# Rows of AUGRU steps 4 to 11: eight gathers of whole rows and a spread by plain DMAs, in place of 32 gathers of quarter rows; other PSUM banks for the first AUGRU products

## The chip, the cores and the metric

One core of a Trainium2 chip runs the whole program in one launch. The metric is the device time in microseconds (us). The kernel before takes 2016.64 us (median of 3 runs, 2015.94 to 2016.9). Its profiled execution, from which every row below comes, has a span of 1995.2 us from its first to its last instruction.

Engines are named as in the profile: PE (TensorE), DVE (VectorE), ACT (ScalarE), POOL (GpSimd, which also issues the indirect DMAs) and SP (SyncE, which here issues all other DMAs but two).

## The reference

A recommender of the DIEN kind: a GRU over 100 steps, an attention over its states, a second GRU whose update gate is scaled by the attention (AUGRU), and a small network at the end. The batch is 1024, every width is 128.

```python
_, gru_seq = jax.lax.scan(gru_step, h0, jnp.swapaxes(item_historical_embedding, 0, 1))
keys = jnp.swapaxes(gru_seq, 0, 1)                       # (1024, 100, 128)
q = jnp.broadcast_to(item_embedding[:, None, :], keys.shape)
feat = jnp.concatenate([keys, q, keys - q, q * keys], axis=-1)
score = _mlp(feat, [(att_W0, att_b0), (att_W1, att_b1), (att_W2, att_b2)], jax.nn.relu)
score = jnp.where(mask[:, :, None] == 1, score, -jnp.inf)
attn = jax.nn.softmax(score, axis=1)[..., 0]
pooled = jnp.einsum('bt,btd->bd', attn, keys)
att_seq = pooled.T[:T]                                   # row t: one weight for each batch entry

def augru_step(h, inp):
    x_t, a_t = inp
    ti = jnp.concatenate([h, x_t], axis=-1)
    r = jax.nn.sigmoid(ti @ aug_Wr.T + aug_br)
    u = jax.nn.sigmoid(ti @ aug_Wu.T + aug_bu)
    h_hat = jnp.tanh(jnp.concatenate([h * r, x_t], axis=-1) @ aug_Wh.T + aug_bh)
    u = a_t[:, None] * u
    h_new = (1.0 - u) * h + u * h_hat
    return (h_new, h_new)
_, aug_seq = jax.lax.scan(augru_step, h0, (jnp.swapaxes(keys, 0, 1), att_seq))
idx = (sequential_length - 1)[:, None, None]
attention_feature = jnp.take_along_axis(jnp.swapaxes(aug_seq, 0, 1), idx, axis=1)[:, 0, :]
```

The AUGRU reads at step t the state of the first GRU at step t (its key, `x_t`) and one attention weight for each batch entry (`a_t`). Only the state at a sequence's last step is used, so a sequence that has ended need not be carried further.

## The kernel before, in words

The 1024 batch columns are two halves of 512. Instructions stand in each engine's queue in the order in which the program writes them (`manual_schedule`); each engine takes its own queue in order, and waits at an instruction until the semaphores that it needs have come.

**First phase** (`gru_phase`, 0 to about 1406 us). 100 GRU steps for both halves, with attention scores, the softmax and the pooling beside them. The states are transposed in 32x32 blocks into tiles `kt` and stored to DRAM tables `keys_d[q]`: `keys_d[0]` holds steps 0 to 3, each further one eight steps (`keys_d[1]`: steps 4 to 11). The batch entries are ranked by length meanwhile.

**Second phase** (`augru_phase`, from about 1406 us to the end). The batch is now in the order of the ranks, so that the columns in use shrink from 510 at step 1 to a few at the end. A step is taken for half 0 and then half 1 (`half_step(t, i)`, written (t, i) below). For (t, i) the PE closes three products that were opened with the key (`open_gates`, L1264) by adding the state's part (`close_gate`, L1268): `pr`, `pu`, and later `ph` with r*h. ACT makes the sigmoids (L1292, L1293) and the tanh (L1276), DVE the products: r*h (L1300), u times the attention weight `at` (L1305), (u-1)*h (L1308), and in the next half step the new state (L1298, L1302).

Three kinds of data have to arrive by DMA:

- **keys.** The rows of `keys_d[q]` are gathered in rank order by indirect DMAs of 128 rows. For steps 0 to 3 a gathered row is one batch entry. For the later ones a gathered row is a quarter of an entry (32 of the 128 features of 8 steps, 1 KB), placed so that DVE can transpose it by 32x32 blocks into a key (`load_key`, L1253). 16 gathers serve a half's eight steps. For steps 4 to 11 half 0's are issued in three lots (four at step T-2, four after the loop, eight at the end of the phase), half 1's sixteen after the gathers of the attention weights. The keys of step 4 are read at (3, 0) and (3, 1).
- **attention weights of steps 1 to 3** (`chosen`). They come from a product on the PE; `store_chosen` copies them (L1199) and SP stores them to DRAM (`att_d<-att_t`, L1200) and loads them back, spread over the partitions (`at<-att_d`, L1228), for steps 2 and 3.
- **attention weights of the later steps.** SP stores the pooled features (`pooled_d<-pooled`, L1146); POOL gathers them in rank order (`att_r`, L158); DVE masks them (L1206), PE transposes them (`pw`, L1213), and SP stores and loads them in the same way (L1216, L1228).

Every DMA that SP issues has one of eight semaphores in turn, and the framework lets it wait until the DMA eight places before it has landed; the same holds for POOL's indirect DMAs with eight others.

PSUM has eight banks. In the second phase seven of them go round in a ring (`NEXT_BANKS`, then `LATE_BANKS`); the products of (1, 0) take `LATE_BANKS` by name, the first copy of weights takes `SPARE`. A bank is free for them when its last use in the first phase has ended, which for some is the DVE's pooling at the very end (L699, L700).

## Time and profile before

| | |
|---|---|
| time of the timed runs, median (lowest to highest) | 2016.64 us (2015.94 to 2016.9) |
| profiled execution, first to last instruction | 1995.2 us |
| difference of the two, outside the instructions | 21.4 us |
| PE busy, share of the span | 1980.5 us, 99% |
| DVE, ACT, POOL busy | 1673.4, 940.7, 1262.7 us |
| PE's share of the chain that ended last | 98% |
| indirect DMAs of rows (L193) | 218, 972 ns of POOL each |
| SP's DMAs of the weights `at<-att_d` (L1228) | 196, 319 to 589 ns of issue each |

How to read it. A row of the timeline has its start in us from the first instruction, its duration in us, the engine, the line, the operation, what it writes and reads, and the count of instructions merged into it; in square brackets stands how long the engine sat idle before it, and what ended that. SPq is SP issuing a DMA: its duration is that of the issue and not of the transfer. A row of waits has the engine and line that waited, on whom, the total in us, the number of times and the longest. A row of the table by stretches has the stretch, then each engine's busy time in it, the granted PE clock, the mean busy share of the 16 DMA engines and GB/s.

### The profile page before, as it was taken

The page shows a single profiled execution, that of the slowest core. Times are in us where ns is not written, and L with a number is a line of the kernel's source. Part 1 is how long each engine was busy: PE and PEld are TensorE (multiplying, and loading weights), DVE is VectorE, ACT ScalarE, POOL GpSimd, SP SyncE. Part 2 cuts the span into 40 slices and gives each one's busy share as a digit, 9 for nine tenths or more (in the row PEclk, how much of TensorE's full clock was granted, in tenths as well). Part 3 has the DMA queues.
Part 4 walks back from the last instruction along what each step waited for, and adds up shares of the span by engine and source line. Part 5 has one row for each costly group of instructions (what it writes and reads, how often), then busy time and mean ns, then how long its engine had stood idle before and what let it go on. Part 6 is the DMA issues. An engine that isn't in the chain of part 4 may idle for free.

```text
span 1995.2 us, 40926 instructions
## 1 busy us (share of the span) xinstructions
PE 1980.5 (99%) x15324; PEld 877.7 (44%) x15324; DVE 1673.4 (84%) x3036; ACT 940.7 (47%) x1689; POOL 1262.7 (63%) x1300
## 2 busy tenths in 40 slices
PE   9999999999999999999999999999999999999998
PEld 2333333333333333333333333334444556678997
DVE  7888999887979898888888798998687778888995
ACT  4444454454544444544545444446334444445553
POOL 0333939669796959496796858898763354445331
PEclk9999999999999999999999999999999999999999
DMA  4443333223334434332343333332543333333331
GB/s 125 99 119 92 108 105 102 89 84 108 116 104 113 116 99 134 111 106 85 103 129 108 93 107 108 92 108 67 155 146 92 96 111 97 93 103 100 83 81 35
DMA packets 244572, 205.59 MB, mean 103 GB/s; under 512 B 61811, under 2 KB 207068, under 8 KB 244364
## 3 DMA queue, kind: packets, MB, share of 16 engines
q1 hardware_dynamic: 231852, 170.31, 29.5%
q0 software_dynamic: 12224, 32.05, 5.7%
q8 instruction: 122, 2.00, 0.4%
q14 instruction: 86, 0.70, 0.1%
q10 hardware_dynamic: 288, 0.52, 0.1%
HBM read 146.75 MB, written 54.42 MB: 101 GB/s over the span
## 4 chain that ended last, share of the span: by engine, by line
PE 98%; DVE 1%; ACT 0%; issue 0%; ACTq 0%; DVEq 0%
PE ps L588 51%; PE pm L770 18%; PE ph L1268 5%; PE pr L1264 4%; PE pu L1264 4%; PE ph L1264 4%; PE pu L1268 4%; PE pr L1268 4%; PE last L737 1%; PE pr L1359 0%; PE ph L1359 0%; PE p L1479 0%; ACT pr L1378 0%; PE pd L248 0%; DVE r L1386 0%
## 5 line engine op out<-in xcount | busy, mean ns | idle before, releaser
L588 PE MATMUL ps<-x,wih 128*32 128x512 f32 x4800 | 603.2, 593 | 0.0
L588 PE MATMUL ps<-hn,whh 128*32 128x512 f32 x4752 | 597.1, 592 | 0.0
L588 PEld LDWEIGHTS ps<-x,wih 128*32 128x32 f32 x4800 | 175.6, 110 | 342.7 <-issue 338.1
L588 PEld LDWEIGHTS ps<-hn,whh 128*32 128x32 f32 x4752 | 173.7, 110 | 338.2 <-issue 335.6
L600 ACT ACTIVATE r<-ps,brz 128x512 f32<-128x512 f32 x200 | 137.5, 688 | 381.3 <-PE ps L588 381.1
L573 POOL TENSOR_TENSOR xm<-x,m 128x512 f32<-128x512 f32 x200 | 233.3, 1167 | 66.7 <-DMA m<-mask_d 66.5
L574 POOL TENSOR_TENSOR hist<-hist,xm 128x512 f32<-128x512 f32 x200 | 258.2, 1291 | 15.7
L193 POOL DMA_INDIRECT rows<-keys_d,idx_k x218 | 212.0, 972 | 84.0 <-POOL rows L192 69.2
L700 POOL TENSOR_TENSOR pooled<-pooled,kw 128x512 f32<-128x512 f32 x192 | 245.5, 1279 | 15.1
L699 POOL TENSOR_TENSOR kw<-kt,e 128x512 f32<-128x512 f32 x192 | 206.3, 1074 | 67.9 <-DVE e L888 67.9
L621 ACT ACTIVATE ps<-ps,bih 128x512 f32<-128x512 f32 x198 | 131.1, 662 | 228.4 <-DVE ps L618 228.4
L770 PE MATMUL pm<-hn,wk 128*32 128x512 f32 x1200 | 215.0, 592 | 0.0
L770 PE MATMUL pm<-kq,wkq 128*32 128x512 f32 x1200 | 214.9, 592 | 0.0
L1276 ACT ACTIVATE c<-ph,bh 128x510 f32<-128x510 f32 (+57 forms) x174 | 88.3, 507 | 252.0 <-PE ph L1268 251.5
L608 DVE SCALAR_TENSOR_TENSOR u<-ps,bhh,r 128x512 f32<-128x512 f32 x198 | 147.4, 744 | 68.5 <-PE ps L588 66.3
L770 PE MATMUL pm<-mv,w 128*32 128x512 f32 (+1 forms) x808 | 194.9, 592 | 0.1
L631 DVE TENSOR_TENSOR d<-hn,ps 128x512 f32<-128x512 f32 x198 | 136.0, 687 | 36.0 <-ACT ps L621 35.7
L618 DVE TENSOR_TENSOR ps<-ps,u 128x512 f32<-128x512 f32 x200 | 140.0, 700 | 24.1 <-PE ps L588 3.1
L642 ACT COPY hn<-ps 128x512 f32<-128x512 f32 x198 | 115.4, 583 | 92.5 <-DVE kq L637 90.8
L632 DVE TENSOR_TENSOR d<-ps,d 128x512 f32<-128x512 f32 x198 | 136.9, 691 | 26.2 <-ACT ps L622 11.0
L192 POOL COPY rows<-rest 128x1 f32<-128x1 f32 x186 | 35.0, 188 | 192.8 <-DVE rest L1308 191.1
L1298 DVE TENSOR_TENSOR pu<-pu,c 128x510 f32<-128x510 f32 (+57 forms) x173 | 81.9, 473 | 77.8 <-ACT c L1276 75.5
(271 smaller groups left out, 3138.9 us busy)
## 6 DMA issues: line engine op xcount, KB each, us to landing
x<-in_hist_x SPq DMA_DIRECT2D x210, 256.0 KB
keys_d<-kt SPq DMA_DIRECT2D x48, 1024.0 KB
m<-mask_d SPq DMA_DIRECT2D x200, 128.0 KB
rows<-keys_d,idx_k POOLq DMA_INDIRECT x218, 3.0
s_b<-mv SPq DMA_DIRECT2D x200, 8.0 KB
keys_d<-kt SPq DMA_DIRECT2D x32, 64.0 KB
mask_i<-in_mask SPq DMA_DIRECT2D x8, 200.0 KB
part_d<-part SPq DMA_DIRECT2D x2, 400.0 KB
```

Source lines behind the costliest of these rows:

```text
L193: nc.gpsimd.indirect_dma_start(out=r[:, at, :], out_offset=None, in_=keys_d[q], in_offset=bass.IndirectOffsetOnAxis(ap=idx_k[:, k, i : i + ...
L573: nc.gpsimd.tensor_mul(d, x, m)
L574: nc.gpsimd.tensor_add(acc, acc, d)
L588: nc.tensor.matmul(p[ts(q, R), :], lhsT=w[:, g, ts(q, R)], rhs=v, start=(j == 0), stop=(j == len(parts) - 1),)
L600: nc.scalar.activation(r, pr, AF.Sigmoid, bias=brz[:, 0:1])
L608: nc.vector.scalar_tensor_tensor(out=u, in0=ph, scalar=bhh[:, 2:3], in1=r, op0=ALU.add, op1=ALU.mult,)
L618: nc.vector.tensor_add(pi, pi, u)
L699: eng.tensor_mul(d, k, w)
L700: eng.tensor_add(acc, acc, d)
L770: nc.tensor.matmul(p[i][s, :], lhsT=w[:, s], rhs=v, start=start, stop=stop)
L1264: nc.tensor.matmul(p, lhsT=m[:, 1, :], rhs=k, start=True, stop=False)
L1268: nc.tensor.matmul(p, lhsT=m[:, 0, :], rhs=v, start=False, stop=True)
```

## The change

Five things change.

1. `keys_d[1]` is laid out by whole batch entries (row: 8 steps x 128 features, 4 KB), where it was by quarters. `store` writes it with four DMAs (one for each 32 partitions) where it was one.
2. The 16 gathers of half 0 for steps 4 to 11 become four gathers of 128 whole rows (512 KB each), all after the pooling, into tiles `pair`. `spread_rows` then moves each gathered tile to the places that DVE reads, by 16 DMAs from SBUF to SBUF of 32 partitions x 1 KB, issued by SP: 64 DMAs.
3. The same for half 1: gathers of groups 0 and 1 stand before the gathers of the attention weights and are spread at once (32 DMAs of SP), those of groups 2 and 3 after them, spread at (2, 0) (32 more). They go through two buffers (`st3`).
4. `LATE_BANKS` is (4, 0, 5) and no longer (2, 4, 5), `SPARE` is 2 and no longer 0, and the ring has bank 2 where bank 0 was. The ring is the same but for the names of three banks.
5. The tile `part3` of the last prediction has one buffer (room for `st3`).

```diff
--- before.py
+++ after.py
@@ -75,7 +75,7 @@
 WIDTHS = [[max(LEAST, n) for n in alive] for alive in ALIVE]
 
 FREE = 134 * 256
-LATE_BANKS, SPARE, NEXT_BANKS = (2, 4, 5), 0, (6, 3, 1, 0)
+LATE_BANKS, SPARE, NEXT_BANKS = (4, 0, 5), 2, (6, 3, 1, 2)
 
 PR = P // NH
 BQ = B // (P // R)
@@ -115,7 +115,7 @@
     dram = ctx.enter_context(tc.tile_pool(name="dram", bufs=1, space=DRAM))
 
     keys_d = [
-        dram.tile([B, n * P] if q < WHOLE else [NK * P, n * R], F32, name=f"keys_d{q}")
+        dram.tile([B, n * P] if q <= WHOLE else [NK * P, n * R], F32, name=f"keys_d{q}")
         for q, n in enumerate(READ)
     ]
@@ -164,6 +164,21 @@
 
     rows = {}
 
+    def part_of(q, i, k):
+        some = rows[q, i]
+        part, at = divmod(k, KH // len(some))
+        return some[part], at
+
+    def spread_rows(i, g, whole):
+
+        to, at = part_of(WHOLE, i, g * P // R)
+        for k in range(P // R):
+            for p in range(P // R):
+                nc.sync.dma_start(
+                    out=to[ts(p, R), at + k, :],
+                    in_=whole[ts(k, R), ts(p, READ[WHOLE] * R)],
+                )
+
     def load_rows(q, i, width, tiles):
 
         n = READ[q]
@@ -179,14 +194,14 @@
             tiles.tile([P, KH // parts, n * R], F32, tag=tag, name="rows") for _ in range(parts)
         ]
         rows[q, i] = some
+        if q == WHOLE:
+            return
         for k in range(-(-width // R)):
             load_row(q, i, k)
             yield
 
     def load_row(q, i, k):
-        some = rows[q, i]
-        part, at = divmod(k, KH // len(some))
-        r = some[part]
+        r, at = part_of(q, i, k)
         if later.get("pace") is not None:
 
             nc.gpsimd.tensor_copy(r[:, at, 0:1], later["pace"])
@@ -666,6 +681,16 @@
 
             def store(self, q):
                 row, part = divmod(q - WHOLE, 2)
+                if row == 0:
+                    to = keys_d[WHOLE][self.cols, :].rearrange(
+                        "(k r) (p m) -> p r k m", r=R, p=P // R
+                    )
+                    for p in range(P // R):
+                        nc.sync.dma_start(
+                            out=to[p][:, :, ts(part, G * R)],
+                            in_=self.kt[q][ts(p, R)].rearrange("p k n c -> p k (n c)"),
+                        )
+                    return
                 nc.sync.dma_start(
                     out=keys_d[WHOLE + row].rearrange("(k p) m -> p k m", p=P)[
                         :, self.ks, ts(part, G * R)
@@ -929,12 +954,6 @@
 
         rest = load_later()
         early = [load_rows(0, i, HB, mid) for i in range(NH)]
-        more_early = load_rows(1, 0, HB, kx)
-
-        def gather_early(n):
-            for _ in range(n):
-                next(more_early)
-
 
         late, again, early_from = 6, 24, 84
         for s in range(T):
@@ -1001,8 +1020,6 @@
                 if last:
                     half.cross_features()
 
-            if s == T - 2:
-                gather_early(4)
             for half in halves:
                 half.pool(2 if len(half.todo) > 7 or s >= 92 else 1, nc.gpsimd)
                 if s >= GATHER:
@@ -1026,7 +1043,6 @@
             for f in these:
                 next(features[f])
 
-        gather_early(4)
         some(0, 1)
         take(T - 2)
         for half in halves:
@@ -1148,7 +1164,15 @@
                 )
         halves[0].kt[q] = kept
         halves[0].store(q)
-        all_of(more_early)
+        all_of(load_rows(WHOLE, 0, HB, kx))
+        wholes = []
+        for g in range(GH):
+            if g % 2 == 0:
+                pair = kp.tile([P, 2, READ[WHOLE] * P], F32, tag="kt", name="pair")
+            wholes.append(pair[:, g % 2, :])
+            gather(wholes[g], keys_d[WHOLE], g, 0)
+        for g in range(GH):
+            spread_rows(0, g, wholes[g])
 
     def augru_phase(pools, widths, alive):
 
@@ -1157,6 +1181,7 @@
         qp = pools.enter_context(tc.tile_pool(name="qp3", bufs=4 * NH))
         wp = pools.enter_context(tc.tile_pool(name="wp3", bufs=3))
         sp = pools.enter_context(tc.tile_pool(name="sp3", bufs=2))
+        st = pools.enter_context(tc.tile_pool(name="st3", bufs=2))
         kp = pools.enter_context(tc.tile_pool(name="kp3", bufs=4))
 
         minus = [wp.tile([P, P], F32, name=f"minus{j}", bufs=1) for j in range(2)]
@@ -1430,7 +1455,7 @@
                     in_offset=i and bass.IndirectOffsetOnAxis(ap=idx_p[:, g : g + 1], axis=0),
                 )
 
-            part = sp.tile([P, M0], F32, tag=f"part_{tag}", name="part3")
+            part = sp.tile([P, M0], F32, tag=f"part_{tag}", name="part3", bufs=1 if last else 2)
             rows_of(part, part_d, None, True)
             yield
             f0 = sp.tile([MC, n, P], F32, name="f0")
@@ -1545,11 +1570,24 @@
         chosen = [later["chosen", i] for i in range(NH)]
         keys.update({(1, i): later["key", 1, i] for i in range(NH)})
         open_gates(1, 0, ("pr", "pu"), LATE_BANKS)
+        all_of(load_rows(WHOLE, 1, HB, kp))
+
+        wholes = {}
+
+        def gather_wholes(*groups):
+            for g in groups:
+                wholes[g] = st.tile([P, READ[WHOLE] * P], F32, name="whole")
+                gather(wholes[g], keys_d[WHOLE], g, 1)
+
+        def spread_wholes(*groups):
+            for g in groups:
+                spread_rows(1, g, wholes.pop(g))
+
+        gather_wholes(0, 1)
+        spread_wholes(0, 1)
         sorted_rows = [gather_weights(i) for i in range(NH)]
-        ahead = load_rows(1, 1, widths[FIRST[1]], kp)
-        for _ in range(P // R):
-            next(ahead)
-        due = spread_over(-(-widths[FIRST[1]] // R) - P // R, NH * (FIRST[1] - 2))
+        gather_wholes(2, 3)
+        due, ahead = [], iter(())
         jobs, final = [], None
         for t in range(1, T):
             if t == one:
@@ -1563,6 +1601,8 @@
                     half_step(t, i)
                 elif i == 0:
                     whole_step(t)
+                if (t, i) == (2, 0):
+                    spread_wholes(2, 3)
                 for _ in range(due.pop(0) if due else 0):
                     next(ahead, None)
 
```

The order of SP's queue, where the first phase ends and the second begins (`pooled_d` is the store of the pooled features, `keys_d_72` that of the last block of states, `pair` and `whole` are the gathered tiles, `att_d`/`at` are the attention weights). Before:

```order
L669 DMA keys_d_72<-kt 128x16x128
L1620 UNCONDITIONAL_BRANCH
L1623 COMPARE_AND_BRANCH
L1200 DMA att_d_78<-att_t 4x512
L1228 DMA at<-att_d_78 128x506
L1228 DMA at<-att_d_78 128x500
L1200 DMA att_d_79<-att_t 4x512
L1228 DMA at<-att_d_79 128x506
L1228 DMA at<-att_d_79 128x500
L1216 DMA att_d_78<-att_t 96x512
```

And now:

```order
L694 DMA keys_d_72<-kt 128x16x128
L177 DMA rows<-pair 32x256 x64
L1660 UNCONDITIONAL_BRANCH
L1663 COMPARE_AND_BRANCH
L177 DMA rows<-whole 32x256 x32
L1225 DMA att_d_78<-att_t 4x512
L1253 DMA at<-att_d_78 128x506
L1253 DMA at<-att_d_78 128x500
L1225 DMA att_d_79<-att_t 4x512
L1253 DMA at<-att_d_79 128x506
L1253 DMA at<-att_d_79 128x500
L177 DMA rows<-whole 32x256 x32
```

Before, the store of the first weights (`att_d_78<-att_t 4x512`) stood directly behind the last store of the first phase, but for two branches; now 96 DMAs `rows<-pair` and `rows<-whole` stand between them, and 32 more before the store of the later weights.

POOL's queue, behind the last pooling of the first phase (`rows` are the gathers of quarter rows, `att_r` those of the weights). Before:

```order
L700 TENSOR_TENSOR pooled<-pooled,kw 128x16x28
L193 DMA rows<-keys_d_61,idx_k 128x256 x8
L1619 TENSOR_LOAD over_d
L1620 UNCONDITIONAL_BRANCH
L1623 COMPARE_AND_BRANCH
L1696 ISA
L158 DMA att_r<-pooled_d,idx 128x128
```

And now:

```order
L725 TENSOR_TENSOR pooled<-pooled,kw 128x16x28
L158 DMA pair<-keys_d_61,idx 128x1024 x4
L1659 TENSOR_LOAD over_d
L1660 UNCONDITIONAL_BRANCH
L1663 COMPARE_AND_BRANCH
L1736 ISA
L158 DMA whole<-keys_d_61,idx 128x1024
L1736 ISA
L158 DMA whole<-keys_d_61,idx 128x1024
L1736 ISA
L158 DMA att_r<-pooled_d,idx 128x128
```

Eight gathers `rows` of half 0 (and eight more earlier in the queue, not shown here) have become four gathers `pair`, and two gathers `whole` of half 1 have come ahead of the gathers `att_r`.

POOL's queue, at the last gathers `att_r` in the second phase. Before:

```order
L158 DMA att_r<-pooled_d,idx 128x128
L1696 ISA
L158 DMA att_r<-pooled_d,idx 128x128
L193 DMA rows<-keys_d_61,idx_k 128x256 x16
L192 COPY rows<-rest 128x1
L193 DMA rows<-keys_d_62,idx_k 128x256
```

And now:

```order
L1736 ISA
L158 DMA att_r<-pooled_d,idx 128x128
L1736 ISA
L158 DMA att_r<-pooled_d,idx 128x128 x3
L158 DMA whole<-keys_d_61,idx 128x1024 x2
L207 COPY rows<-rest 128x1
L208 DMA rows<-keys_d_62,idx_k 128x256
```

Sixteen gathers of quarter rows of half 1 have become two gathers of whole rows; behind them the gathers for steps 12 to 19 follow in both. The PE's, DVE's and ACT's queues keep their order.

## The prediction

> **What bounds the kernel now.** I read the page first: its busy times and its chain.
>
> ```profile
> PE 1980.5 (99%) x15324; PEld 877.7 (44%) x15324; DVE 1673.4 (84%) x3036; ACT 940.7 (47%) x1689; POOL 1262.7 (63%) x1300
> PE 98%; DVE 1%; ACT 0%; issue 0%; ACTq 0%; DVEq 0%
> ```
>
> The PE is busy almost throughout, so the change can gain only where the PE waits or runs slowly, and can lose wherever it makes the PE wait. The waits of the PE give the place, and the timeline around it (PE, DVE) the detail.
>
> ```profile
> PE pr L1264 <- DVE last L699: 2.8, 1, 2.8
> ...
> 1403.23 0.69 ACT L1105 ACTIVATE s_b<-last,bh 128x512 f32<-128x512 f32 x1
> ...
> 1408.88 0.62 DVE L699 TENSOR_TENSOR last<-kt,last 128x448 f32<-128x448 f32 x1
> 1409.64 1.93 PE L1264 MATMUL pr<-hist,wr 128*128 128x510 f32 x2 [2.83 <-DVE last L699]
> 1411.37 1.91 PE L1264 MATMUL pu<-hist,wu 128*128 128x510 f32 x2
> 1412.04 0.63 DVE L699 TENSOR_TENSOR last<-kt,last 128x448 f32<-128x448 f32 x1
> 1413.07 1.08 PE L1268 MATMUL pr<-h_all,wr 128*128 128x510 f32 x2
> 1418.74 1.02 PE L1268 MATMUL ph<-r,wh 128*128 128x510 f32 x2
> ```
>
> The PE's longest wait, 2.83 us, is at the seam of the phases: `pr` of (1, 0) takes a bank that DVE's pooling reads until 1409.50. After it the PE is slow. The table by stretches (columns: PE, PEld, DVE, ACT, POOL busy, then granted clock, DMA share, GB/s) shows why:
>
> ```profile
> 1410.00:1412.00 2.00, 2.00 (x3) 0.69 (x3) 1.93 (x4) 0.00 (x0) 1.39 (x3) 0.50 0.41 115
> 1412.00:1414.00 2.00, 2.00 (x5) 0.79 (x4) 1.25 (x3) 0.00 (x0) 1.61 (x2) 0.71 0.46 131
> ```
>
> The granted clock was 0.50 there. The first four products took 1413.07 - 1409.64 = 3.43 us, where the pairs behind them take 0.86 each: 1.7 us were lost to the clock.
>
> **The banks.** In the new order of banks `pr` of (1, 0) takes a bank last read by ACT's L1105, done at 1403.9, and `pu` one that the softmax left earlier still. So they can run where the wait began (1409.64 - 2.83 = 1406.8), at the full clock, and end at 1408.5. But `ph` of (1, 0) stays in bank 5, which the last L699 reads until 1412.67. `pr`, `pu` closed and `row` (three pairs, 2.6 us) fill the PE until 1411.2; it waits 1.5 us, and then `ph` (0.86), a transpose (0.48), and `pr`, `pu` of (1, 1) (1.72) bring the closing of `ph` to 1415.8 instead of 1418.9, where the chain has it (the row says 1418.74 with the overlap). The gain offered is 3.1 us.
>
> **The gathers.** POOL issues 24 gathers fewer. Their pitch:
>
> ```profile
> 1406.67 0.99 POOL L193 DMA_INDIRECT rows<-keys_d,idx_k  x1
> 1407.96 0.95 POOL L193 DMA_INDIRECT rows<-keys_d,idx_k  x1 [0.30 <-issue]
> ...
> 1418.98 0.94 POOL L158 DMA_INDIRECT att_r<-pooled_d,idx  x1 [2.56 <-issue]
> ...
> 1447.81 0.95 POOL L193 DMA_INDIRECT rows<-keys_d,idx_k  x1 [0.30 <-issue]
> ```
>
> 24 x 1.25 = 30 us of POOL. I price this at nothing: POOL isn't on the chain, at the end of the phase the saved time runs into the wait for the pooled store (2.56 us before `att_r`), and what it covered was only that half 1's last row was issued at 1447.81 and read at 1451.55.
>
> **The spread, on SP.** This is the term that decides. SP issues in order. Before, the first weights went out as soon as they were ready and were back before DVE asked:
>
> ```profile
> 1415.34 0.49 SPq L669 DMA_DIRECT2D keys_d<-kt  x1
> ...
> 1424.77 0.26 SPq L1200 DMA_DIRECT2D att_d<-att_t  x1
> 1426.60 0.82 SPq L1228 DMA_DIRECT2D at<-att_d  x2
> 1429.20 0.27 SPq L1200 DMA_DIRECT2D att_d<-att_t  x1
> 1430.89 0.80 SPq L1228 DMA_DIRECT2D at<-att_d  x2
> 1441.67 0.32 SPq L1216 DMA_DIRECT2D att_d<-att_t  x1
> 1443.93 0.32 SPq L1228 DMA_DIRECT2D at<-att_d  x1
> ```
>
> Now 96 DMAs (64 of half 0, 32 of half 1) stand between 1415.9 and that store. Behind it are the loads of `at` for steps 2 and 3, and DVE's L1305 of (2, 0) waits for the first of them, then everything. No row shows a spread DMA, so I bound its pitch on SP by the nearest rows: a pair of loads of `at` takes 0.82 (0.41 each); these two are the only DMA from SBUF to SBUF, and the only burst from 32 partitions:
>
> ```profile
> 1392.60 1.11 SPq L825 DMA_DIRECT2D s_b<-mv  x2
> ...
> 1406.93 1.04 SPq L1146 DMA_DIRECT2D pooled_d<-pooled  x2
> ```
>
> That is 0.53 to 0.56 each. The first moves 4 rows and the second 512 pieces, and a spread 32 rows of 1 KB, simpler than either; the shortest issue of all is the 0.26 of the weights' store above. Ends: 0.26 and 0.56. I take 0.45, between the loads and the burst.
>
> Each SP DMA also waits for the one eight places before it. Landing is about 1.8 us (the store of 1424.77 releases the load of 1426.60), and eight issues at 0.45 take 3.6, so in steady state the issue sets the pace. Only the eighth spread is held: it waits for the 1 MB store of 1415.34, and the DMA engines are full until about 1421:
>
> ```profile
> 1418.00:1420.00 2.00, 2.00 (x6) 0.84 (x5) 0.00 (x0) 0.20 (x1) 0.94 (x1) 1.00 1.13 347
> 1420.00:1422.00 2.00, 2.00 (x6) 0.95 (x5) 1.35 (x3) 1.64 (x3) 1.47 (x2) 1.00 0.49 143
> ...
> 1426.00:1428.00 2.00, 2.00 (x6) 0.47 (x4) 0.00 (x0) 0.00 (x0) 1.39 (x3) 1.00 0.22 69
> 1428.00:1430.00 2.00, 1.33 (x7) 0.69 (x6) 0.00 (x0) 0.66 (x2) 1.60 (x2) 1.00 0.81 247
> ```
>
> With 3 MB of gathered rows in front I put it at 1422. So the store of the weights is issued at 1422 + 88 x 0.45 = 1461.6; the load 1.83 later; and the load lands some 3.3 us after its issue (its half megabyte is what fills the DMA engines from 1428 to 1430): 1466.7.
>
> What DVE has to do from there, and when the PE takes it up:
>
> ```profile
> 1433.57 0.68 DVE L1305 TENSOR_TENSOR pu<-pu,at 128x506 f32<-128x506 f32 x1
> 1434.29 0.68 DVE L1308 SCALAR_TENSOR_TENSOR rest<-pu,h_all 128x506 f32<-128x506 f32 x1
> 1434.89 0.55 DVE L1206 TENSOR_TENSOR att_r<-att_r,used_s 128x384 f32<-128x384 f32 x1
> 1437.02 0.69 DVE L1298 TENSOR_TENSOR pu<-pu,c 128x506 f32<-128x506 f32 x1 [1.58 <-ACT c L1276]
> 1437.84 0.68 DVE L1300 TENSOR_TENSOR r<-h_all,pr 128x506 f32<-128x506 f32 x1
> ...
> 1440.75 1.01 PE L1268 MATMUL ph<-r,wh 128*128 128x506 f32 x2
> ```
>
> L1305 of (2, 0) ran at 1433.57 unhindered. In the stall the PE and ACT do all that needs no weight, so afterwards only DVE's own five instructions (3.3 us) stand before the PE closes `ph` of (2, 1): 1470.1, against 1440.75. That is 29.3 us. The PE restarts at half clock, 1.7 us by the rows of the seam: 31.0. The 3.1 us of the banks are inside this and gain nothing, since the stall's end is set by SP and not by the PE.
>
> **The second spread.** Groups 2 and 3 of half 1 use the buffers of groups 0 and 1, so POOL gathers the last when the 96th spread has landed; SP issues six DMAs of weights (6.9 us, as before from 1424.77 to 1431.69), then 32 spreads (14.4), and only then the later weights. The rows of half 1 are there at 1461.6 + 6.9 + 14.4 + 1.8 = 1484.7; the first weights of step 4 at 1461.6 + 6.9 + 14.4 + 0.1 + 2.3 (store to load) + 3.3 = 1488.6. They are read here, 31.0 later:
>
> ```profile
> 1451.55 0.71 DVE L1253 STREAM_TRANSPOSE k<-rows 128x512 f32<-128x512 f32 x1
> 1452.99 0.69 DVE L1298 TENSOR_TENSOR pu<-pu,c 128x500 f32<-128x500 f32 x1 [0.73 <-ACT c L1276]
> ...
> 1454.97 0.67 DVE L1305 TENSOR_TENSOR pu<-pu,at 128x496 f32<-128x496 f32 x1
> ...
> 1457.98 0.68 DVE L1298 TENSOR_TENSOR pu<-pu,c 128x496 f32<-128x496 f32 x1 [0.95 <-ACT c L1276]
> ```
>
> 1482.5 for the rows: 2.2 late, 0.7 of it idle time of DVE, so 1.4 more. Then 1487.4 for the weights: 1.2 late, 0.95 idle, 0.3 more.
>
> **The rest.** SP's own waits in the first phase:
>
> ```profile
> SPq L825 <- ACT mv L818: 839.2, 94, 13.1
> ```
>
> The two stores of `keys_d[1]`, now eight DMAs each, stand in the steps about 8 and 12 there, where SP waits this long in all and loads two steps ahead: nothing, and if that cover were gone 12 more DMAs x 0.55 = 7 us. The single buffer of `part3`: nothing. Half 0's rows (64 spreads) land before 1450 and are read one half step ahead of half 1's.
>
> **The sum.** 29.3 + 1.7 + 1.4 + 0.3 = 32.7 us. Span 1995.2 + 32.7 = 2027.9; the timed median lies 21.4 above the span, so 2016.64 + 32.7 = 2049.3 us. The ends by the same sum: pitch 0.26 gives +14.3 (2031), 0.37 +24 (2041), 0.53 +42 (2059), 0.56 +46 (2062.5).
>
> **The rivals.**
> - *The issue is quick, and the landing sets the pace.* At 1.8 us of landing and eight in flight, a spread needs no more than 0.23 to 0.26, and if SP issues simple DMAs as fast as the lone small store (0.26), the stall is 14 to 24 us: 2031 to 2041. For it: that row; a spread is plain. Against: the store is alone, and every row of two or more DMAs in a run has 0.41 or more. The Trainium skill (DMA: Bandwidth & Descriptors, Issuing engines are not separate DMA queues) says that the sequencer's time to start a DMA is usually small beside the DMA itself, which would put this rival first. The rows agree only in part: 0.41 to 0.56 against 1.8 is a quarter, and with eight in flight that isn't small. The same page (Rules for kernel authors) advises to join small transfers, those under 64 KB being mostly overhead, and this change cuts 512 KB into pieces of 32 KB: that speaks against it as the forecast does.
> - *The issue is slow.* At the burst's 0.53 to 0.56, or if reading 32 partitions at a time makes the landing longer than 8 x 0.5 = 4 us, the second spread is late too: 2059 to 2075. For it: both rows nearest in kind. Against: they move odd pieces.
> - *Faster: the spread hides.* Then the PE keeps the 3.1 us of the banks: 2013.5. It needs the weights on DVE at 1433.57 - 3.1 = 1430.5, so their store at 1425.4, so 88 spreads in 3.4 us, 0.04 each: it decides at a pitch six times below the shortest issue in the trace. Only another order of SP's work than the one shown could do it.
> - *Nothing happens*, gain and loss both small: nothing in the rows speaks for it.
>
> **How the numbers follow.** Forecast (pitch 0.37 to 0.53, 2041 to 2059) 0.55; quick issue 0.20; slow issue 0.17; faster 0.05; within 0.2% (about what a measurement of this kernel can tell from no change) 0.03. The range 2031 to 2066 takes in the forecast, nearly all of the quick case and more than half of the slow one: about 0.84. Slower by over 0.2%: 0.55 + 0.20 + 0.17 = 0.92.
>
> **What would show it.** In the profile after: SP's L177 in an unbroken run from about 1416 to about 1461, its 96 issues at 0.45; the store L1225 behind it; DVE's L1330 of (2, 0) waiting some 30 us for the DMA `at<-att_d`; an empty PE there and a granted clock of 0.50 behind it; `pr` of (1, 0) at 1406.9 with no wait for L724, and a short one for `ph`; small waits at (3, 1) and (4, 0). POOL's row gathers for steps 12 to 19 start as much later as the steps do. The prediction is wrong if the first weights are back before DVE asks, or if the loss stands elsewhere: in DVE waiting for rows, in POOL waiting for a buffer, in PSUM banks.

## The result, and the profile after

The changed kernel takes 2060.88 us (median of 5 runs, 2059.93 to 2061.4) against 2016.9 us before (5 runs, 2015.94 to 2018.39): the ratio is 1.0218, 95% interval 1.0207 to 1.023, so it is 44 us slower. The prediction said 2049 (2031 to 2066). The time lies in the range, but two of the numbers behind it were wrong, with opposite signs: that it still lies there is luck. This part and the experiments show both.

The first sign is the profiled span: 2058.1 us against 1995.2, which is 62.9 more and not 44. The times lie 1.8 us above their spans in this kernel, where the prediction had found 21.4 before. From the page of the changed kernel (busy times, and shares of the chain that ended last):

```profile
PE 1985.4 (96%) x15324; PEld 878.9 (43%) x15324; DVE 1671.9 (81%) x3036; ACT 940.7 (46%) x1689; POOL 1241.7 (60%) x1276
PE 93%; SPq 4%; issue 1%; DVE 1%; ACT 0%; DMA 0%; POOL 0%; DVEq 0%; ACTq 0%; POOLq 0%
```

The PE's work is nearly the same (1985 us against 1981), its share of the chain fell from 98% to 93%, and SP's queue, which was not on the chain at all, has 4%. The waits of the PE in the changed kernel (us in total, times, longest):

```profile
PE pw L1238 <- issue: 51.0, 1, 51.0
PE pr L1289 <- DVE k L1278: 6.5, 1, 6.5
```

Two long waits where there was one of 2.83 us. SP's queue in the changed kernel (start, duration, and how many) shows what made them:

```profile
1415.78 2.37 SPq L694 DMA_DIRECT2D keys_d<-kt  x1
1418.25 42.08 SPq L177 DMA_DIRECT2D rows<-pair  x64
1460.55 20.39 SPq L177 DMA_DIRECT2D rows<-whole  x32
1481.04 0.43 SPq L1225 DMA_DIRECT2D att_d<-att_t  x1
1482.64 0.83 SPq L1253 DMA_DIRECT2D at<-att_d  x2
...
1487.53 21.20 SPq L177 DMA_DIRECT2D rows<-whole  x32
```

The 96 spreads run without a break from 1418.25 to 1480.94, and the store of the first weights stands behind them, at 1481.04 instead of 1424.77. DVE's side of it, in the timeline of DVE (in brackets the idle time before, and what ended it):

```profile
1486.12 0.69 DVE L1330 TENSOR_TENSOR pu<-pu,at 128x506 f32<-128x506 f32 x1 [55.83 <-DMA at<-att_d]
...
1487.45 0.55 DVE L1231 TENSOR_TENSOR att_r<-att_r,used_s 128x384 f32<-128x384 f32 x1
...
1510.18 0.71 DVE L1278 STREAM_TRANSPOSE k<-rows 128x512 f32<-128x512 f32 x1 [8.17 <-DMA rows<-whole]
...
1514.27 0.68 DVE L1330 TENSOR_TENSOR pu<-pu,at 128x496 f32<-128x496 f32 x1 [1.65 <-DMA at<-att_d]
```

The view of the PE's waits finds no releaser for the 51.0 (`issue`), but the rows do: `pw` reads `att_r`, which DVE's L1231 masks, and L1231 stands in DVE's queue behind L1330. It ended at 1488.00, and `pw` starts at 1488.10.

To see how much each wait costs, the same products of the PE are set side by side. After:

```profile
1488.10 1.06 PE L1238 MATMUL pw<-ident,att_r 128*96 128x128 f32 x4 [50.98 <-issue]
...
1496.75 1.00 PE L1293 MATMUL ph<-r,wh 128*128 128x500 f32 x2
...
1510.95 2.02 PE L1289 MATMUL pr<-k,wr 128*128 128x496 f32 x2 [6.52 <-DVE k L1278]
...
1517.40 1.00 PE L1293 MATMUL pr<-h_all,wr 128*128 128x496 f32 x2
```

And in the profile before:

```profile
1440.32 0.60 PE L1213 MATMUL pw<-ident,att_r 128*96 128x128 f32 x4
...
1446.23 1.00 PE L1268 MATMUL ph<-r,wh 128*128 128x500 f32 x2
...
1453.75 0.99 PE L1264 MATMUL pr<-k,wr 128*128 128x496 f32 x2
...
1457.07 0.99 PE L1268 MATMUL pr<-h_all,wr 128*128 128x496 f32 x2
```

The lag of the later kernel is 47.8 us at the first of these, 50.5 at the second, 57.2 at the third, 60.3 at the fourth. So the first wait cost 47.8 (it is 51.0 long, but the PE had come to it 3.2 earlier than before) and the slow restart behind it 2.7; the second wait cost 6.7 and its restart 3.1. The stretches of the changed kernel (granted clock third from the end) show the clock at half behind the first wait, at full later, and at half again behind the second:

```profile
1488.00:1490.00 2.00, 1.82 (x5) 1.14 (x6) 1.78 (x3) 0.00 (x0) 0.00 (x0) 0.50 0.74 204
...
1494.00:1496.00 2.00, 2.00 (x6) 0.86 (x5) 1.97 (x4) 0.65 (x1) 0.00 (x0) 1.00 0.20 54
...
1510.00:1512.00 2.00, 1.05 (x2) 0.56 (x3) 1.81 (x4) 0.00 (x0) 0.00 (x0) 0.50 0.26 77
```

The remaining 2.6 us of the 62.9 lie behind these products and are not placed; the spans of one kernel differ by as much from run to run (2015.0 to 2019.7 us in the ten runs of the first experiment).

The banks did what was said of them: at the seam the PE no longer waits for `pr`.

```profile
1406.27 1.09 PE L1289 MATMUL pr<-hist,wr 128*128 128x510 f32 x2
...
1412.27 1.12 PE L1289 MATMUL ph<-hist,wh 128*128 128x510 f32 x2 [1.48 <-DVE last L724]
...
1415.38 1.02 PE L1293 MATMUL ph<-r,wh 128*128 128x510 f32 x2
```

The closing of `ph` moved from 1418.74 to 1415.38, 3.4 us, of which the seam gave 2.9: the PE came to it 0.5 earlier (`first`, its last product ahead of the seam, starts at 1404.38 against 1404.84). It gains nothing, since the wait for the weights follows.

### The profile page after: what moved, and what is told of

The parts are those of the page before. It is cut to its first block, busy times and chain, and to the rows that moved or that the text cites. A ratio compares the mean times of both kernels' runs of the same rounds, so it can differ in the third digit from the quotient of the medians.

```text
span 2058.1 us, 41066 instructions
## 1 busy us (share of the span) xinstructions
PE 1985.4 (96%) x15324; PEld 878.9 (43%) x15324; DVE 1671.9 (81%) x3036; ACT 940.7 (46%) x1689; POOL 1241.7 (60%) x1276
## 4 chain that ended last, share of the span: by engine, by line
PE 93%; SPq 4%; issue 1%; DVE 1%; ACT 0%; DMA 0%; POOL 0%; DVEq 0%; ACTq 0%; POOLq 0%
PE ps L603 50%; PE pm L795 17%; PE ph L1293 4%; PE pr L1293 4%; PE pr L1289 4%; PE pu L1289 4%; PE pu L1293 4%; PE ph L1289 4%; SPq L177 4%; PE pr L1384 0%; PE last L762 0%; PE ph L1384 0%; SPq L1162 0%; DMA att_d<-att_t 0%; PE p L1504 0%
## 5 line engine op out<-in xcount | busy, mean ns | idle before, releaser
L208 POOL DMA_INDIRECT rows<-keys_d,idx_k x186 | 182.0, 978 | 75.5 <-POOL rows L207 47.0
L648 DVE TENSOR_TENSOR ps<-ps,d 128x512 f32<-128x512 f32 x198 | 138.5, 699 | 6.7
```

Source lines behind the costliest of these rows:

```text
L208: nc.gpsimd.indirect_dma_start(out=r[:, at, :], out_offset=None, in_=keys_d[q], in_offset=bass.IndirectOffsetOnAxis(ap=idx_k[:, k, i : i + ...
L648: nc.vector.tensor_add(pi, pi, d)
```

## The experiments

Three questions were open: why 62.9 us of span are 44 us of time, what makes a spread take 0.65 us on SP where 0.45 was taken, and whether the order of SP's queue, or the number of its DMAs, is what costs. Times of kernels are compared only with runs of the kernel before on the same chip.

### The kernel before, once more

No edit.

> The kernel before, unchanged, once more: how does the time stand to the span? The profile shown of it has a span of 1995.2 us and the runs a median of 2016.6, which is 21.4 more; in the changed kernel the two differ by 1.9 us (2058.1 and 2059.93). If what lies outside the span is a constant of the program, the spans of these runs are about 1995 and their times 2016. If instead the profile shown was of a quicker execution than the timed ones, the spans here are about 2014 to 2015, with times about 2 us above them, and some 19 us more of work or wait stand in the trace.

Measured: 2018.81 us (10 runs), beside 2018.64 (21 runs of the same kernel); ratio 1.0002, 0.9993 to 1.0011. The profiled execution has a span of 2015.0 and a time of 2016.81, and every other run too lies 1.7 to 1.9 us above its span. The second case holds: the profile shown of before is of an execution some 20 us quicker than the timed ones. Where these 20 us are, the waits of the PE in this run tell first; then the PE and ACT around them, from the timelines:

```profile
PE pu L1264 <- ACT c L1276: 14.5, 2, 14.0
```

```profile
1434.05 0.60 PE L1246 MATMUL pk<-ident,rows 128*128 128x128 f32 x4
```

```profile
1433.17 0.66 ACT L1293 ACTIVATE pu<-pu,bu 128x506 f32<-128x506 f32 x1 [1.60 <-PE pu L1268]
1451.40 0.58 ACT L1247 COPY k<-pk 128x500 f32<-128x500 f32 x1 [17.57 <-remote]
```

ACT's copy of `pk` needs only the PE's transposes, which by the record were over at 1434.65. It starts at 1451.40. In the profile shown before, the same copy is

```profile
1435.45 0.58 ACT L1247 COPY k<-pk 128x500 f32<-128x500 f32 x1 [2.32 <-PE pk L1246]
```

So there is a stall of some 16 us, in which everything that ACT waits for is done by the records of the PE. What ended the wait is `remote` in the row: an update of a semaphore for which the view finds no instruction. The trace file of the run also holds the times at which the semaphore that the PE raises was updated. In the profile shown before, each of these updates around the copy stands within 0.02 us of its product's end, and the copy starts at 1435.45, behind the update of 1435.43. Here there is none between 1433.15 and 1444.39, then come 1444.39, 1447.17, 1449.28, 1450.68 and 1451.37, and the copy starts 0.03 us behind the last. So ACT itself was ready: it waited for the PE's signal, and the signal came late. (Ends of products are modelled in the trace; a PE that was itself held up would look the same.) The stall lies in the time in which POOL gathers the 16 quarter rows of half 1 (1428.2 to 1448.0 in this run), and the changed kernel has no such gathers there.

### Only the banks

```
-LATE_BANKS, SPARE, NEXT_BANKS = (2, 4, 5), 0, (6, 3, 1, 0)
+LATE_BANKS, SPARE, NEXT_BANKS = (4, 0, 5), 2, (6, 3, 1, 2)
```

> The kernel before with only the new order of banks. Theory: the PE's wait of 2.83 us at pr of the first AUGRU step goes, a wait of 1.5 us comes at ph, and the half clock behind goes; the span is 3.1 us shorter, 0.15% of the time (ratio 0.9985). Rival: the last row of half 1, gathered at 1447.81 and read at 1451.55, comes too late by up to 2 us and gives most of it back: ratio 0.9995 or above. A second rival: PE waits as long for DVE elsewhere, and nothing is gained.

Measured: 2016.67 us (11 runs) against 2018.64; ratio 0.9989, 0.998 to 0.9998. That is 2.0 us, 0.4 to 4.0 by the interval. The 3.1 of the theory are inside, but so is the 1 us of the first rival (ratio 0.9995), so the time does not decide between them. The long stall of ACT is here as well, split in several pieces; first the waits of the PE, then the first piece in the timeline of ACT:

```profile
PE pu L1264 <- ACT c L1276: 10.5, 1, 10.5
PE ph L1268 <- DVE r L1300: 2.9, 2, 2.7
PE ph L1264 <- DVE last L699: 1.5, 1, 1.5
```

```profile
1441.01 0.58 ACT L1247 COPY k<-pk 128x500 f32<-128x500 f32 x1 [11.42 <-issue]
```

The wait of 2.83 at `pr` is gone, and the 1.5 at `ph` stands in its place, as foreseen. From `first` to the closing of `ph` it is 11.0 us (1404.20 to 1415.20), where the profile shown before has 13.9 (1404.84 to 1418.74).

### Only the gathers and the spread

```
-LATE_BANKS, SPARE, NEXT_BANKS = (4, 0, 5), 2, (6, 3, 1, 2)
+LATE_BANKS, SPARE, NEXT_BANKS = (2, 4, 5), 0, (6, 3, 1, 0)
```

> The changed kernel with the old order of banks: only gathers and spread are changed. Theory: the end of the stall is set by SP's queue, so the 3 us of the banks were swallowed and the time is that of the changed kernel within 1 us (about 2060). Rival: the banks count on top, and it is 3 us slower (about 2063).

Measured: 2060.89 us (4 runs) against 2018.64; ratio 1.0211, 1.0196 to 1.0227. That is the changed kernel's 2060.88 again, on a chip whose kernel before is 1.7 us slower; 3 us more would have been a ratio of 1.0233, outside the interval. Its waits of the PE:

```profile
PE pw L1238 <- issue: 48.9, 1, 48.9
PE pr L1289 <- DVE k L1278: 6.7, 1, 6.7
PE pr L1289 <- DVE last L724: 2.8, 1, 2.8
```

The 2.8 at the seam is back, and the long wait is shorter by 2.1: its end is set by SP. The theory holds; what the banks gain is swallowed. But there was less to swallow in this profile than the 3.1 of the forecast. Behind the same wait the products ran at the full clock, where the profile shown before has 1.93 us for this row:

```profile
1409.05 1.09 PE L1289 MATMUL pr<-hist,wr 128*128 128x510 f32 x2 [2.83 <-DVE last L724]
```

From `first` to the closing of `ph` it is 12.2 us here, only 1.2 more than with the new banks.

### One DMA for a group in place of sixteen

```
-        for k in range(P // R):
-            for p in range(P // R):
-                nc.sync.dma_start(
-                    out=to[ts(p, R), at + k, :],
-                    in_=whole[ts(k, R), ts(p, READ[WHOLE] * R)],
-                )
+        nc.sync.dma_start(
+            out=to[:, at : at + P // R, :],
+            in_=whole.rearrange("p (k m) -> p k m", k=P // R),
+        )
```

> The changed kernel with one DMA for each gathered group, of 128 partitions by 4 KB, in the place of 16 of 32 partitions by 1 KB. It copies the same bytes straight and leaves the spread over the quarters out, so the output is another. 6 DMAs stand before the first weights instead of 96. Theory (a fixed cost of about 0.63 us for each DMA on SP): 4 us of issue, which end before the weights are ready at 1424.8; no stall for the weights, span about 1992 to 1996, time as before or 3 us less. Rival (the cost goes with the rows, 0.63/32 = 20 ns each): 2.5 us for each DMA, the six end at about 1434, and the stall is about 8 us. Second rival (it goes with the bytes): 10 us each, and the stall stays at 51 us.

Measured: 2000.45 us (4 runs) against 2018.64; ratio 0.9909, 0.9894 to 0.9925. The durations on SP decide between the three; first those of the changed kernel (ns, shortest, median, longest), then those of this one, then its SP queue:

```profile
L177 SPq DMA_DIRECT2D rows<-pair x64: 3/589/2165, 1418.2 to 1459.7; - x64
```

```profile
L175 SPq DMA_DIRECT2D rows<-pair x4: 542/1010/3062, 1418.8 to 1423.3; - x4
L175 SPq DMA_DIRECT2D rows<-whole x4: 470/858/1325, 1424.9 to 1441.0; - x4
```

```profile
1418.79 5.91 SPq L175 DMA_DIRECT2D rows<-pair  x4
1424.91 2.58 SPq L175 DMA_DIRECT2D rows<-whole  x2
1427.58 1.32 SPq L1223 DMA_DIRECT2D att_d<-att_t  x1
```

A spread of 32 x 1 KB has a median of 0.589 us, and all but a few of the 64 lie within 0.02 of it. A DMA of 128 x 4 KB, sixteen times the bytes and four times the rows, can be out in 0.54 and 0.47, where the rivals had 2.5 and 10. So the cost goes neither with the rows nor with the bytes: where nothing else holds it up, it is 0.5 to 0.6 us for each DMA, as the first theory has it. Four of the eight took longer, 1.2 to 3.1 us. They stand where the DMA engines were full (shares of 1.01 to 1.18 from 1412 to 1432 in the stretches of this run), but so do two of the short ones, so that this is why is not shown. The weights were stored at 1427.58, and in the timeline of DVE

```profile
1439.23 0.69 DVE L1328 TENSOR_TENSOR pu<-pu,at 128x506 f32<-128x506 f32 x1 [7.15 <-DMA at<-att_d]
```

is a wait for them, so the guess of no stall was wrong by that. And yet this kernel is 18 us faster than the one before: it has no row gathers of half 1, and in its trace no ACT stall (the PE's longest wait is 2.2).

### The weights ahead of half 1's spreads

```
         gather_wholes(0, 1)
-        spread_wholes(0, 1)
         sorted_rows = [gather_weights(i) for i in range(NH)]
-        gather_wholes(2, 3)
...
+                if (t, i) == (1, 1):
+                    spread_wholes(0, 1)
+                    gather_wholes(2, 3)
                 if (t, i) == (2, 0):
                     spread_wholes(2, 3)
```

> The changed kernel with the 32 spreads of half 1's groups 0 and 1 moved on SP's queue from before the first weights to behind them (and POOL's gathers of groups 2 and 3 behind these). Nothing is left out. Theory (SP has 128 spreads of 0.63 us, 81 us, to issue in a stretch in which the rows and weights are wanted within 33 us, so the order only moves the wait): the first stall is shorter by 32 x 0.63 = 20 us (the weights are back at about 1466 instead of 1486), the rows of half 1 still come at about 1510 or a little later, and the time stays at 2060 within 5 us. Rival (what costs is only that the first weights are late): 20 us faster, about 2040.

Measured: 2059.45 us (2 runs) against 2017.46; ratio 1.0208, 1.0189 to 1.0227. From its timeline of SP, and the waits of the PE:

```profile
1461.08 0.32 SPq L1225 DMA_DIRECT2D att_d<-att_t  x1
...
1467.46 40.92 SPq L177 DMA_DIRECT2D rows<-whole  x64
```

```profile
PE pw L1238 <- issue: 29.3, 1, 29.3
PE pr L1289 <- DVE k L1278: 27.4, 1, 27.4
```

The first wait is 21.7 us shorter than the changed kernel's 51.0, and the second 20.9 longer than its 6.5. The theory holds: with 128 DMAs of 0.65 us on one queue, the order only says where the PE waits.

### Half 0's spreads on ACT's queue

```
+    def spread_rows(i, g, whole, queue=nc.sync):
...
+                queue.dma_start(
...
-            spread_rows(0, g, wholes[g])
+            spread_rows(0, g, wholes[g], nc.scalar)
```

> The changed kernel with the 64 spreads of half 0 issued by ACT instead of SP; nothing is left out. Theory (0.63 us is time of the issuing engine, not of the transfers): both engines keep 0.63 while they issue side by side, SP's 32 are out at about 1439 and ACT's 64 at about 1458; ACT's own work for the first steps waits behind them, so the first stall ends some 10 us earlier than in the changed kernel, time about 2045 to 2052. Rival (what lies behind the queues sets the pace): the two share it, each needs about twice as long for one while both issue, and nothing is gained: 2060 or more.

Measured: 2052.41 us (2 runs) against 2017.46; ratio 1.0173, 1.0155 to 1.0192. The total is at the edge of what the theory said, but the way there was another. The first row is from the timeline of ACT, the second of SP:

```profile
1413.60 43.61 ACTq L177 DMA_DIRECT2D rows<-pair  x64
```

```profile
1454.11 20.49 SPq L177 DMA_DIRECT2D rows<-whole  x32
```

The two hardly issued side by side. SP's waits in this stretch (us, times, longest) say that it was held by ACT's DMAs:

```profile
SPq L177 <- DMA rows<-pair: 25.2, 1, 25.2
SPq L1162 <- DMA rows<-pair: 16.3, 4, 11.8
```

The PE's longest wait is now one for ACT (44.5 us), whose work for the first steps stands behind its 64 issues. So whether two engines share the pace was not tested, and that question stays open. What the run shows is that ACT needs as long for a spread as SP, 43.61 / 64 = 0.68 us, so the price is not one of SP.

### Whole rows without a spread: the PE turns them

The rows are gathered straight into the tiles that are read; `keys_d[1]` is stored so that one step of a whole row is 128 values in a row, and the PE transposes them.

```
+    def gather_whole(i, g):
+        dst = whole_rows(i, g).rearrange("p k m -> p (k m)")
+        gather(dst, keys_d[WHOLE], g, i)
...
+            elif q == WHOLE:
+                p = pa.tile([P, HB], F32, tag="a", name="pk3")
+                for g in range(-(-w // P)):
+                    src = whole_rows(i, g).rearrange("q k m -> q (k m)")
+                    nc.tensor.transpose(p[:, ts(g, P)], src[:, ts(m, P)], ident)
+                nc.scalar.copy(k[:, :w], p[:, :w])
```

> Whole rows are gathered as in the changed kernel, straight into the tiles that are read, all eight gathers ahead of those of the weights, and there is no spread: for steps 4 to 11 PE transposes the rows (four 128 x 128 transposes for a half step) and ACT copies them, where DVE transposed them. The rows of keys_d[1] are stored step by step for it (64 small stores of SP in the first phase). Nothing is left out. Theory: no stall for the weights, and the stall that the timed executions of the kernel before have at 1433 to 1452 goes with its row gathers, as in the kernel with one DMA for each group; against that 16 x 0.48 = 7.7 us of PE. 2000 + 8 = 2008, less or more 5: ratio 0.993 to 0.998. Rival: that stall has nothing to do with the row gathers and stays: 2015 + 8 = 2023, slower than before. Second rival: the one PSUM buffer of the transposes makes PE wait for ACT's copies, 0.6 each, and it is about 2017.

Measured: 2007.98 us (5 runs) against 2017.46; ratio 0.9953, 0.994 to 0.9967. It is 9.5 us below the kernel before on this chip, and the first theory's number (2008) is met. The rival of the single PSUM buffer is small: in the waits of the PE

```profile
PE pk L1269 <- ACT k L1270: 1.3, 2, 0.7
```

is all that ACT's copies cost.

### Four gathers for sixteen

The kernel before, and half 1's rows gathered in 4 instead of 16 DMAs.

```
-        ahead = load_rows(1, 1, widths[FIRST[1]], kp)
-        for _ in range(P // R):
-            next(ahead)
...
+        for g in range(GH):
+            gather(
+                r[:, ts(g, P // R), :].rearrange("p k m -> p (k m)"),
+                keys_d[1].rearrange("(b x) m -> b (x m)", x=P // R),
+                g,
+                1,
+            )
```

> The kernel before, with half 1's 16 row gathers behind those of the weights (128 x 1 KB each, 1429 to 1448) replaced by 4 gathers of 128 x 4 KB: the same bytes, but not spread, so steps 4 to 11 of half 1 read wrong rows. Nothing else is changed. It tests the stall of 16 to 19 us at 1433 to 1452 that the timed executions of before have, where ACT starts 17 us after PE had finished what it waits for. Theory (the long run of row gathers makes it): the stall goes, about 2000 us, ratio 0.991. Rival (it comes from what runs before 1430, or from the bytes): the stall stays, ratio 0.998 or above. In between: part of it stays.

Measured: 2001.71 us (4 runs) against 2017.46; ratio 0.992, 0.9904 to 0.9935, or 15.8 us. In the timeline of ACT the copy that had waited 17.57 us reads now

```profile
1438.40 0.57 ACT L1247 COPY k<-pk 128x500 f32<-128x500 f32 x1 [2.39 <-PE pk L1246]
```

and the PE's longest waits are 2.8 (the seam) and 2.5. So the stall of the kernel before belongs to the run of 16 row gathers, and the same bytes in four gathers don't make it. That removing them removes it is shown; by what way they delay the PE's signal to ACT is not.

### Sixteen gathers of a quarter of the partitions, and the changed kernel on other chips

The four gathers of 128 x 4 KB cut into 16 of 32 x 4 KB, to tell the number of rows from the number of gathers:

```
+            for p in range(P // R):
+                nc.gpsimd.indirect_dma_start(
+                    out=r[ts(p, R), ts(g, P // R), :].rearrange("p k m -> p (k m)"),
...
+                    in_offset=bass.IndirectOffsetOnAxis(
+                        ap=idx[:R, g, 3:4], axis=0
+                    ),
+                )
```

> The kernel with four gathers of 128 x 4 KB for half 1, each of them cut into four gathers of 32 x 4 KB: 16 gathers again at POOL's pitch of 1.25 us, as in the kernel before (to about 1448), but 512 rows and 2 MB as with the four. Half 1 reads wrong rows in steps 4 to 11. Theory (the number of rows, each of them a piece of its own in the DMA queues, makes the stall of the kernel before): no stall, about 2001 us as with the four gathers. Rival (the number of gathers, or POOL's issuing for 20 us on end, makes it): the stall is back, about 2017 us. In between would say that both count.

Measured: 1996.43 us (9 runs), but beside it the kernel before took 1996.37 (11 runs), where on the two chips of the runs above it took 2018.64 and 2017.46. No execution of it there was below 2015 us, and none here above 2000. The stall is not of the program alone: this chip does not show it, and the profile that was shown of before is one without it. The trace files differ too. Of the updates of the PE's semaphore, 2222 in the kernel before, the files of all nine runs profiled on chips with the stall lack 132 to 164, whether their kernel stalls or not; the profile shown before and those on the two chips without a stall lack at most two. So these chips also differ in how an execution is recorded, and whether they would stall without the recording is not shown. With no stall to take away, nothing can be told of rows and gathers. The last three runs went to a fourth chip:

> The changed kernel, once more, beside a kernel before that took 2017 us on two chips and 1996 us on a third. Theory (the 20 us are a stall of the kernel before that only some chips show, and the changed kernel's long wait stands in its place): the changed kernel takes about 2060 us whatever the chip, so +43 us (ratio 1.021) where the kernel before takes 2017, and +63 us (1.032) where it takes 1996. Rival (the third chip is quicker at everything): ratio 1.021 on either.

> The kernel with whole gathers and PE's transposes once more. Theory: where the kernel before takes 2017 us, 2008 again (0.9955); where it takes 1996, there is no stall to take away and the 7.7 us of transposes count against 3 us of the banks: about 2001, slower by 0.2 to 0.4%. Rival: it is 0.5% faster on either.

> The 16 gathers of 32 x 4 KB once more; half 1 reads wrong rows in steps 4 to 11. Where the kernel before takes 2017 us it tells: number of rows (theory) about 2001, number of gathers (rival) about 2017. Where the kernel before takes 1996 both give 1996, as the first time, and it stays open.

Measured there: the kernel before 1996.6 us (14 runs); the changed kernel 2056.92 (4 runs), ratio 1.0297, 1.028 to 1.0314; the kernel whose PE turns the rows 2003.26 (5 runs, about 2001 expected), ratio 1.0033, 1.0019 to 1.0048; the 16 small gathers 1995.93 (10 runs, one of them at 5442.99, which is left out of the ratio), ratio 0.9995, 0.9985 to 1.0005. So the changed kernel costs 60 us (63 were expected) where the kernel before has no stall and 44 us where it has one, and its own time is nearly the same on both. Its trace on this chip (waits of the PE) has the two waits of the first:

```profile
PE pw L1238 <- issue: 51.2, 1, 51.2
PE pr L1289 <- DVE k L1278: 7.6, 1, 7.6
```

The kernel with PE's transposes is slower here by 0.33%, as its expectation said for such a chip (0.2 to 0.4%): the 7.7 us of transposes are more than the banks give. Of the kernels that leave nothing out, only the change of the banks alone is not known to be slower than the one before on some chip, and it was timed on one.

## Why the prediction was right or wrong

**Right: the direction, and the mechanism with its places.** SP's queue holds 96 DMAs ahead of the first weights, DVE's L1330 of (2, 0) waits for `at<-att_d`, the PE stands empty and restarts at half clock. From the store to DVE the forecast had 1466.7 - 1461.6 = 5.1 us, and it took 1486.12 - 1481.04 = 5.1.

**Wrong: the pitch, "I take 0.45, between the loads and the burst", and its upper end of 0.56.** The pitch was (1480.94 - 1418.25) / 96 = 0.65, above both ends. 0.59 of it is the issue itself. With 88 spreads behind the eighth this term alone is 88 x 0.20 = 17.6 us; the store went out 19.4 late by the forecast. The nearest neighbour in kind was among the rows of the prediction: L825, from SBUF to SBUF, 0.56 a piece. The forecast went below it, towards the loads from DRAM, and no neighbour moved 32 rows of 1 KB. The lone store of 0.26, on which the rival of the quick issue was built, was no measure either. The part of the working that said "in steady state the issue sets the pace" was right: it is not the landing. The last spread of half 1 is out at 1487.53 + 21.20 = 1508.73 and DVE reads it at 1510.18, 1.45 us later, and eight spreads take 5.2.

**Wrong in size: the second spread, 1.4 + 0.3 us.** It was 8.17 + 1.65 of DVE's time and 6.7 + 3.1 of the PE's. The working was right and the pitch was not: with 0.65 its sum has the rows there at 1481.0 + 6.9 + 32 x 0.65 + 1.8 = 1510.5, and they were read at 1510.18. The 1.7 for a restart at half clock was low (2.7), and the second restart (3.1) was not in the sum. With 0.65 and nothing else changed, the prediction's own sum gives a loss of some 57 us.

**Wrong: "the timed median lies 21.4 above the span".** This was taken for a constant around the span (the table ahead of the prediction has it as "outside the instructions"). It is 1.7 to 1.9 in every run of the experiments; the other 19.6 were a stall in the timed executions which the profile shown did not have. The step that prices the 24 gathers at nothing fell with it: on a chip with the stall, the row gathers of half 1 cost 15.8 us (four gathers for sixteen), and the changed kernel gets about as much back (62.9 us of span against 44 of time). On a chip without the stall nothing speaks against pricing them at nothing: the PE's longest wait in the profile of before is the 2.8 at the seam.

So the sum had +32.7 in place of +60 to +63 us of span, and did not have the 16 to 20 us that the change saves on the chip on which it was timed. 2049 against 2061 looks like a pitch that was a little low; it is a loss that was nearly twice as large, and a gain that no row of the profile of before showed (only its gap of 21.4 hinted at it). That the range held is luck: 2016.64 and the 57 us of the working with the true pitch are 2074, above its upper end. On a chip without the stall the same forecast, counted from that chip's 1996.6, would have been 2029, 28 below what was measured.

**The rivals.** The quick issue is refuted by the 0.59. The slow issue (0.53 to 0.56, with the second spread late too, 2059 to 2075) was the right one, and its pitch was still low. What the Trainium skill (DMA: Bandwidth & Descriptors, Issuing engines are not separate DMA queues) says, that the time to start a DMA is usually small beside the DMA itself, does not hold here: 0.59 to issue and 1.45 to land. Its advice to join small transfers (the same page, Rules for kernel authors) does: six DMAs in place of 96 gave 2000.45, where the 96 gave 2060.89 on the same chip with the old banks (the six copy straight, so they show the price and are no replacement). "Faster: the spread hides" asked for 0.04 a piece and is out.

**Banks and covers.** The 3.1 us offered were 2.9 in the trace and 2.0 (0.4 to 4.0) when timed alone. The 1.7 of them that were put down to the half clock are not there in every execution: behind the same wait of 2.83 us the clock stayed full in two of six traces. That the gain is swallowed here is shown by the kernel without the new banks. The twelve more stores of `keys_d[1]` cost nothing, as said: `pr` of (1, 0) starts at 1406.27, no later than the 1406.8 of the forecast.

## What to carry to other kernels

Count the DMAs on a queue, not their bytes: 128 small ones at 0.65 us are 83 us of an engine's time, and whatever is behind them in order waits, so that an order only moves the wait; a transfer that replaces a slow gather has to be joined into few, or be done by an engine that is there anyway. For an operation of which no row shows the price, the nearest rows are guesses, and the range should reach well above the dearest of them.

Before a sum is made from a profile, ask whether its execution is like the timed ones: a gap of 20 us between span and time, where all other runs have 2, was here a stall that the profile did not show. And a change that takes or gives one per cent should be timed on more than one chip.

## What the runs showed of the hardware that was not expected

- A plain DMA of 32 x 1 KB from SBUF to SBUF takes the issuing engine 0.59 us on SP and 0.60 on ACT, and one of 128 x 4 KB can take as little (0.47 to 0.54).
- The same program has a stall of 16 to 20 us on two chips (every timed run of the kernel before over 2015 us) and none on two others (every one below 2000). In the stall ACT starts a copy 16.7 us after the PE had finished its input by the record, and 0.03 us after the PE's semaphore was updated, so it waited for that signal. Four gathers in place of a run of sixteen take the stall away (15.8 us). The trace files from chips with the stall lack 132 to 164 of some 2222 updates of this semaphore, those from the others at most two. What in these chips, in the hours in which they were used, or in the recording makes the difference, and whether it is the number of gathers or of their rows, stays open: both runs that should tell it met chips without the stall.
- The granted clock was 0.50 after a wait of the PE of 6.5 us, and never below 1.00 behind the wait of 1.48 us at the seam. Behind the same wait of 2.83 us it was one or the other: it fell to 0.5 in four traces (the profile shown before, the kernel before once more, the four gathers, the 16 small gathers the second time) and stayed at 1.00 in two (the changed kernel with the old banks, the 16 small gathers the first time). From `first` to the closing of `ph` this makes 12.2 us or 13.7 to 15.3.
